# Storing the second sample of the last tile by 16 transfers of falling width

## The chip, the cores and the metric

The kernel runs on one core of one Trainium2 chip. The metric is the device time of one execution in microseconds (us); before the change it is 1864.5 us, the median of two runs (1864.28 and 1864.72). The span in the profile, from the first to the last instruction, is a little shorter: 1862.7 us.

## What is computed

For 1024 samples, `xi` and `xj` each hold 39 fields of 16 numbers. Every one of the 741 pairs (row above column) gets the outer product of two fields, 16 by 16; it is normalised with the mean and variance over all samples and all 256 products of the pair, and multiplied by a 16 by 16 weight.

```python
rows, cols = np.tril_indices(39, k=-1)                       # 741 pairs
cross = xj[:, rows, :, None] * xi[:, cols, None, :]          # 1024 x 741 x 16 x 16
mean = jnp.mean(cross, axis=(0, 2, 3), keepdims=True)
var = jnp.mean(jnp.square(cross - mean), axis=(0, 2, 3), keepdims=True)
normed = (cross - mean) * jax.lax.rsqrt(var + 1e-5)
normed = normed * gamma[None, :, None, None] + beta[None, :, None, None]
out = normed[:, :, None, :, :] * W[None, None, :, :, :]
```

The output is 1024 x 741 x 256 numbers of four bytes, 777 MB; the inputs are 6 MB. So the work is above all the writing of the output.

## The kernel before

Each of the 128 partitions holds eight samples, since 1024 = 128 x 8. A *tile* is `(r, t0, u)`: all `r` pairs of row `r` for two samples `t0` and `t0 + 1` of every partition (`T = 2`), at place `u` of the big buffer `y_sb`. The list `tiles` (lines 68 to 77) starts with row 19, goes on with row 20, and then takes the rows 38 down to 21, each followed by its complement 38 - r, so that a long and a short row together fill one of two slots of `y_sb`. The last tile is row 17 (the complement of row 21), with `t0 = 6`: 17 pairs of 256 numbers, that is 17,408 bytes per sample and partition, two samples, 4352 KB in all.

At the start, moments of the inputs are gathered (lines 351 to 473) and turned into one scale and one shift per pair. Then the loop of line 521 goes over the tiles: `products` (line 178) forms the outer products on ScalarE and GpSimd, line 148 and 150; `finish` (line 271) adds the shift and multiplies with the weight, on VectorE (line 308) and for a share of the pairs on GpSimd (lines 294 and 297); `store` (line 220) sends a tile or a piece of one to memory. All stores are issued by SyncE from one line, 231, so they enter one queue in the order of the program, and each is worked off by the 16 DMA engines, each of which takes its part of every transfer in that order.

What decides how `store` cuts its transfers: rows above 19 (`mid`) have one transfer per sample, in general; rows up to 19 have `step = T`, one transfer for both samples. The last tile is of the second kind, so its 4352 KB leave in one transfer.

SyncE waits before each issue for the engines that wrote the tile. It waits for one thing more: each transfer reports its completion on a semaphore, eight semaphores are handed out in turn, and so the issue of a transfer waits until the transfer eight places before it in the program has landed. At the very end (line 555 in the profile, the end of the program) SyncE waits until all transfers have landed.

Of the kernel before, what the change touches and what calls it, by code (L numbers as in the profile page):

```python
# [41 lines left out]
def tile_pair_outer_batchnorm(  # L42
# [15 lines left out]
    nc = tc.nc  # L58
# [3 lines left out]
    EE = E * E  # L62
# [7 lines left out]
    tiles = [(mid, t0, t0 // T * half // 2) for t0 in range(0, NT, T)]  # L70
# [25 lines left out]
    out_v = out.rearrange("(p t) o n i j -> p t (o n i j)", t=NT)  # L96
# [41 lines left out]
    def view(n):  # L138
        r, _, u = tiles[n]
        return y_sb[:, u : u + T * r, :].rearrange("p (t n) e -> p t n e", t=T)  # L140
# [79 lines left out]
    def store(n, c0, c1, t_from=0, t_to=T):  # L220
        r, t0, _ = tiles[n]
        n0 = first[r]

        whole = n >= len(FIRST_PIECES) and r <= WHOLE
        step = 1 if r > mid and (whole or c1 == r) else t_to - t_from
        for t in range(t_from, t_to, step):
            if whole and step == 1 and t == t_to - 1:
                if c1 < r:
                    continue
                c0 = 0  # L230
            nc.sync.dma_start(  # L231
                out_v[:, t0 + t : t0 + t + step, (n0 + c0) * EE : (n0 + c1) * EE],
                view(n)[:, t : t + step, c0:c1, :].rearrange("p t n e -> p t (n e)"),
            )

    def affine(n, pairs, engines=(nc.scalar, nc.gpsimd)):

# [11 lines left out]
    def weigh(n):  # L249

        y = view(n)
        for c0, c1 in zip(bounds(n), bounds(n)[1:]):
            affine(n, range(c0, min(c1, OWN)), (nc.vector,))
            nc.vector.tensor_tensor(  # L254
                y[:, :, c0:c1, :],
                y[:, :, c0:c1, :],
                w_dve.unsqueeze(1).to_broadcast([P, T, c1 - c0, EE]),
                ALU.mult,
            )
            store(n, c0, c1)  # L260
# [10 lines left out]
    def finish(n):  # L271
# [33 lines left out]
        for t in range(0, T, size):  # L305
            for c0, c1 in zip(bounds(n), bounds(n)[1:]):
                for c in [*range(c0, min(c1, p0)), *range(max(c0, p1), c1)]:
                    stt(  # L308
                        y[:, t : t + size, c, :],
                        y[:, t : t + size, c, :],  # L310
                        t_sb[:, n0 + c : n0 + c + 1],
                        w_dve.to_broadcast([P, size, EE]),
                        ALU.add,
                        ALU.mult,
                    )
                store(n, c0, c1, t, t + size)
# [243 lines left out]
```

## Time and profile before

| what | value |
|---|---|
| time, median of 2 runs | 1864.5 us |
| span in the profile | 1862.7 us |
| written to memory | 776.99 MB |
| busy: VectorE (DVE), ScalarE (ACT), GpSimd (POOL) | 92%, 85%, 83% of the span |
| last store (4352 KB), from issue to landing | 26.0 us |
| end of the last compute instruction | about 1835.4 us |

The page of the profile names work by engine and line. A DMA engine is not an instruction engine: what the 16 DMA engines do is told by the DMA rows (their mean busy share, and GB/s moved). A DMA share of 1.00 means that all 16 were busy; one of them alone gives 0.06. PEclk is of no matter here, since TensorE works in the first slice only.

### The profile page before, as it was taken

What the parts mean: (1) busy time and instruction counts of PE and PEld (TensorE: products, weight loads), DVE (VectorE), ACT (ScalarE), POOL (GpSimd) and SP (SyncE); (2) the same over time, 40 slices, a digit from 0 to 9 for tenths busy, and PEclk for the clock granted to TensorE, in tenths of its full rate; (3) what the DMA queues carried; (4) which work ended last, traced back from release to release, by engine and by line L of the source; (5) the groups of instructions that cost most, each with busy time, mean ns of one, the idle gap of its engine ahead of it and who ended that gap; (6) DMA issues with size and microseconds to landing.
All of it is one profiled execution on the core that took longest, in us unless ns stands there. A gap on an engine that the chain in (4) does not pass through costs nothing.

```text
span 1862.7 us, 9385 instructions
## 1 busy us (share of the span) xinstructions
PE 34.3 (2%) x212; PEld 33.7 (2%) x212; DVE 1714.3 (92%) x2638; ACT 1576.3 (85%) x3130; POOL 1542.9 (83%) x1655
## 2 busy tenths in 40 slices
PE   7000000000000000000000000000000000000000
PEld 7000000000000000000000000000000000000000
DVE  8999889899999999999999999999999999999994
ACT  8999888888888776666898989999999998989891
POOL 9999777787777789999988888888888888888882
PEclk7555555555555555555555555555555555555555
DMA  7999999999999999999999999999999999999998
GB/s 289 396 421 421 430 427 427 429 424 427 424 428 423 424 424 426 427 425 425 420 428 429 428 430 427 426 427 427 427 431 427 426 428 431 428 425 428 428 428 359
DMA packets 55286, 783.60 MB, mean 421 GB/s; under 512 B 4784, under 2 KB 6448, under 8 KB 18096
## 3 DMA queue, kind: packets, MB, share of 16 engines
q1 hardware_dynamic: 54928, 782.53, 99.2%
q14 instruction: 69, 0.57, 0.1%
q10 hardware_dynamic: 288, 0.48, 0.1%
q8 instruction: 1, 0.02, 0.0%
HBM read 6.00 MB, written 776.99 MB: 420 GB/s over the span
## 4 chain that ended last, share of the span: by engine, by line
DMA 53%; ACT 22%; DVE 18%; issue 3%; POOL 1%; PE 0%; SPq 0%; ACTq 0%; DVEq 0%; POOLq 0%
DMA out_dram<-y_sb 53%; ACT y_sb L148 22%; DVE y_sb L308 17%; POOL y_sb L150 1%; DVE y_sb L364 0%; POOL xs L170 0%; POOL y_sb L247 0%; PE ps L401 0%; SPq L231 0%; DVE y_sb L254 0%; ACTq L148 0%; PE ps L379 0%; DVE y_sb L385 0%; DVE y_sb L371 0%; DVE xs L183 0%
## 5 line engine op out<-in xcount | busy, mean ns | idle before, releaser
L308 DVE SCALAR_TENSOR_TENSOR y_sb<-y_sb,st_sb,w_dve 128x512 f32<-128x512 f32 (+1 forms) x2511 | 1653.1, 740 | 113.3 <-issue 95.9
L148 ACT ACTIVATE y_sb<-xs,xj_sb 128x144 f32<-128x144 f32 (+23 forms) x2930 | 1453.0, 586 | 238.2 <-DMA out_dram<-y_sb 181.6
L297 POOL TENSOR_TENSOR y_sb<-y_sb,w_sb 128x2048 f32<-128x2048 f32 (+3 forms) x155 | 517.4, 3343 | 89.1 <-ACT y_sb L292 79.5
L150 POOL TENSOR_SCALAR y_sb<-xs,xj_sb 128x320 f32<-128x320 f32 (+19 forms) x1006 | 557.4, 577 | 9.8 <-DMA out_dram<-y_sb 9.7
L170 POOL TENSOR_TENSOR xs<-xi_sb,st_sb 128x640 f32<-128x640 f32 (+33 forms) x135 | 183.9, 1362 | 178.8 <-ACT y_sb L148 174.5
L294 POOL TENSOR_SCALAR y_sb<-y_sb,st_sb 128x512 f32<-128x512 f32 x291 | 196.8, 692 | 5.1 <-ACT y_sb L148 5.1
L292 ACT ACTIVATE y_sb<-y_sb,st_sb 128x512 f32<-128x512 f32 x160 | 100.2, 708 | 3.8 <-POOL y_sb L150 2.1
L203 POOL TENSOR_TENSOR y_sb<-xs,xj_sb 128x1280 f32<-128x1280 f32 (+2 forms) x24 | 66.7, 2802 | 0.0
L193 DVE TENSOR_TENSOR y_sb<-xs,ps 128x256 f32<-128x256 f32 (+3 forms) x32 | 24.8, 818 | 0.5
L487 PE MATMUL ps<-y_sb 38*128 38x38 f32 (+37 forms) x76 | 16.4, 397 | 2.4 <-DVE y_sb L473 2.4
L487 PEld LDWEIGHTS ps<-y_sb 38*128 38x128 f32 x76 | 16.3, 329 | 2.5 <-POOL y_sb L150 2.5
L150 POOL TENSOR_SCALAR y_sb<-xi_sb,xj_sb 128x304 f32<-128x304 f32 x24 | 11.9, 514 | 0.0
L254 DVE TENSOR_TENSOR y_sb<-y_sb,w_dve 128x2048 f32<-128x2048 f32 (+4 forms) x6 | 10.8, 1840 | 0.5 <-POOL y_sb L247 0.5
L364 DVE TENSOR_REDUCE y_sb<-y_sb 128x38 f32<-128x608 f32 x14 | 10.4, 781 | 0.0
L247 POOL TENSOR_SCALAR y_sb<-y_sb,st_sb 128x512 f32<-128x512 f32 x9 | 7.0, 786 | 2.2 <-ACT y_sb L148 2.2
L245 ACT ACTIVATE y_sb<-y_sb,st_sb 128x512 f32<-128x512 f32 x9 | 6.5, 803 | 0.3 <-ACT y_sb L148 0.3
L361 ACT ACTIVATE y_sb<-xi_sb 128x608 f32<-128x608 f32 x8 | 5.7, 707 | 1.1 <-DMA xi_sb<-in_r_xi_dram 0.7
L361 ACT ACTIVATE y_sb<-xj_sb 128x608 f32<-128x608 f32 x8 | 5.7, 708 | 1.1 <-DMA xj_sb<-in_r_xj_dram 0.6
L379 PE MATMUL ps<-xi_sb,y_sb 128*128 128x152 f32 x40 | 6.1, 302 | 0.0
L379 PEld LDWEIGHTS ps<-xi_sb,y_sb 128*128 128x128 f32 x40 | 5.8, 202 | 0.0
L401 PE MATMUL ps<-y_sb 128*128 128x128 f32 x24 | 5.5, 428 | 1.0 <-POOL y_sb L319 1.0
L401 PEld LDWEIGHTS ps<-y_sb 128*128 128x128 f32 x24 | 5.2, 331 | 1.0 <-POOL y_sb L319 1.0
(43 smaller groups left out, 50.5 us busy)
## 6 DMA issues: line engine op xcount, KB each, us to landing
out_dram<-y_sb SPq DMA_DIRECT2D x16, 3072.0 KB, 21.9
out_dram<-y_sb SPq DMA_DIRECT2D x20, 2432.0 KB, 12.5
out_dram<-y_sb SPq DMA_DIRECT2D x10, 4608.0 KB, 15.2
out_dram<-y_sb SPq DMA_DIRECT2D x12, 3840.0 KB, 20.8
out_dram<-y_sb SPq DMA_DIRECT2D x16, 2816.0 KB, 22.1
out_dram<-y_sb SPq DMA_DIRECT2D x12, 3584.0 KB, 22.9
out_dram<-y_sb SPq DMA_DIRECT2D x12, 3328.0 KB, 24.3
out_dram<-y_sb SPq DMA_DIRECT2D x15, 2560.0 KB, 12.3
```

The lines of the kernel that those rows point to most:

```text
L148: nc.scalar.activation(y, src, AF.Copy, scale=scale)
L150: engine.tensor_scalar(y, src, scale, 1.0, ALU.mult, ALU.mult)
L170: nc.gpsimd.tensor_tensor(xs, xi_sb[:, t0 : t0 + T, 0:r, :], s_sb[:, :, n0 : n0 + r, :].to_broadcast([P, T, r, E]), ALU.mult,)
L193: nc.vector.tensor_tensor(view(n)[:, t].rearrange("p n (i j) -> p n i j", j=E), xs[:, t].unsqueeze(2).to_broadcast([P, r, E, E]), xj_short ...
L203: nc.gpsimd.tensor_tensor(view(n)[:, t].rearrange("p n (i j) -> p n i j", j=E), xs[:, t].unsqueeze(2).to_broadcast([P, r, E, E]), xj_sb[:, ...
L292: nc.scalar.activation(y[:, :, c, :], y[:, :, c, :], AF.Identity, bias=t_c)
L294: nc.gpsimd.tensor_scalar(y[:, :, c, :], y[:, :, c, :], t_c, 1.0, ALU.add, ALU.mult)
L297: nc.gpsimd.tensor_tensor(y[:, :, c0:c1, :], y[:, :, c0:c1, :], w_sb.unsqueeze(1).to_broadcast([P, T, c1 - c0, EE]), ALU.mult,)
L308: stt(y[:, t : t + size, c, :], y[:, t : t + size, c, :], t_sb[:, n0 + c : n0 + c + 1], w_dve.to_broadcast([P, size, EE]), ALU.add, ALU.mult,)
L361: nc.scalar.activation(squares[x][:, t], sources[x][:, t], AF.Square, scale=scales[x])
L379: nc.tensor.matmul(ps, unit, sources[x][:, t0:t1, :, e : e + q], start=e == 0, stop=e + q == E)
L487: nc.tensor.matmul(ps[:, :, first[r] - n0 : first[r] - n0 + r], pick[:, r - 1, :], stq[:, :, 0:r], start=True, stop=True,)
```

## The change

```diff
+            to = out_v[:, t0 + t : t0 + t + step, (n0 + c0) * EE : (n0 + c1) * EE]
+            of = view(n)[:, t : t + step, c0:c1, :].rearrange("p t n e -> p t (n e)")
+            if n < len(tiles) - 1:
+                nc.sync.dma_start(to, of)
+                continue
+            nc.sync.dma_start(to[:, 0], of[:, 0])
+            p0 = 0
+            for p in (8, *range(15, 0, -1)):
+                nc.sync.dma_start(to[p0 : p0 + p, 1], of[p0 : p0 + p, 1])
+                p0 += p
```

For every tile but the last nothing changes. The last tile's one transfer becomes 17: its first sample goes over all 128 partitions at once; its second sample goes in 16 transfers over 8, 15, 14, 13 and so on down to 1 partitions, which together are the 128. The bytes are the same. What it is for: at the end of the kernel the 16 DMA engines do not all finish at the same moment, and transfers that cover fewer partitions than there are engines can give some engines more and some less of the remaining bytes.

More of the change, by code (lines that the diff above doesn't have):

```diff
@@ L230, in store @@
                 c0 = 0
[L231 to L234, printed above, removed]
+            to = out_v[:, t0 + t : t0 + t + step, (n0 + c0) * EE : (n0 + c1) * EE]
[8 more added lines that the diff above has]
+                p0 += p
     def affine(n, pairs, engines=(nc.scalar, nc.gpsimd)):
```

## The prediction

> **What bounds the kernel now.** I began with the page: span, DMA totals, and the chain of work that ended last.
>
> ```profile
> span 1862.7 us, 9385 instructions
> ...
> DMA packets 55286, 783.60 MB, mean 421 GB/s; under 512 B 4784, under 2 KB 6448, under 8 KB 18096
> ...
> q1 hardware_dynamic: 54928, 782.53, 99.2%
> ...
> DMA out_dram<-y_sb 53%; ACT y_sb L148 22%; DVE y_sb L308 17%; POOL y_sb L150 1%; DVE y_sb L364 0%; POOL xs L170 0%; POOL y_sb L247 0%; PE ps L401 0%; SPq L231 0%; DVE y_sb L254 0%; ACTq L148 0%; PE ps L379 0%; DVE y_sb L385 0%; DVE y_sb L371 0%; DVE xs L183 0%
> ```
>
> The queue of stores fills 99.2% of the time of 16 DMA engines: the kernel is bound by them, and compute matters only where it feeds them. The change touches the last tile alone, so I looked at SyncE's waits and its timeline from 1835 us on, and then at a table of the DMA share by stretches of the end.
>
> ```profile
> SPq L555 <- DMA out_dram<-y_sb: 25.6, 1, 25.6
> ```
>
> ```profile
> 1835.56 0.38 SPq L231 DMA_DIRECT2D out_dram<-y_sb  x1
> ```
>
> The last store is issued at 1835.56, and nothing but DMA is left for 25.6 us. Its bytes would need 4352 KB / 428 GB/s = 10.4 us; the rest is backlog in front of it.
>
> ```profile
> 1852.00:1854.20 2.20, 0.00 (x0) 0.00 (x0) 0.00 (x0) 0.00 (x0) 0.00 (x0) 0.50 0.98 419
> 1854.40:1855.40 1.00, 0.00 (x0) 0.00 (x0) 0.00 (x0) 0.00 (x0) 0.00 (x0) 0.50 0.29 122
> 1855.40:1856.80 1.40, 0.00 (x0) 0.00 (x0) 0.00 (x0) 0.00 (x0) 0.00 (x0) 0.50 0.23 99
> 1857.00:1858.30 1.30, 0.00 (x0) 0.00 (x0) 0.00 (x0) 0.00 (x0) 0.00 (x0) 0.50 0.19 80
> 1858.50:1859.10 0.60, 0.00 (x0) 0.00 (x0) 0.00 (x0) 0.00 (x0) 0.00 (x0) 0.50 0.14 58
> 1859.20:1861.10 1.90, 0.00 (x0) 0.00 (x0) 0.00 (x0) 0.00 (x0) 0.00 (x0) 0.50 0.04 18
> 1861.10:1862.70 1.60, 0.00 (x0) 0.00 (x0) 0.00 (x0) 0.00 (x0) 0.00 (x0) 0.50 0.00 0
> ```
>
> The last two numbers of a row are DMA share and GB/s. Up to 1854.2 all 16 engines work; then the share falls to 0.29, 0.19, 0.14 and about one sixteenth, that is to 4, 3, 2 and 1 engines. In the packet records twelve engines finish between 1854.4 and 1854.9, the other four at 1856.8, 1858.4, 1859.2 and 1861.13. A packet of this store is one partition's 17,408 bytes, and takes 0.651 us (428 GB/s / 16 = 26.75 GB/s an engine). The latest engine is thus ten packets behind, and sets the end: it enters the last store at 1861.13 - 16 x 0.651 = 1850.7, the others near 1844.1. If the whole lag were spread over 16 engines, about 5 us could be had; nothing more is at stake on this side. The records do not say which of the 16 the late ones are.
>
> [...]
>
> **The change part by part.** [...]
>
> *Issue.* SyncE issues 16 more transfers. A store issue takes 0.33 to 0.38 us alone and up to 1.2 us straight after another (median 0.382, longest 1.347 in the answer for line 231), so 16 cost 6 to 19 us. SyncE is idle from 1836 on, and the twelve early engines need the second sample only at 1844.1 + 8 x 0.651 = 1849.3. For the first few transfers this is hidden.
>
> *The added waits.* Eight completion semaphores go round; in the built instruction order of the changed kernel every transfer waits for the one eight before it. Numbering the narrow ones 1 to 16: number 7 (10 partitions) waits for the last store of row 21, which the latest engine finishes at 1850.7. Number 8 (9 partitions) waits for the first sample's transfer, and numbers 9 to 16 for numbers 1 to 8. Behind the waiting issue the rest of the narrow transfers are queued on SyncE, 45 of the 128 partitions, and the end of the program waits for them. The first sample is complete when the latest engine has done it: 1850.7 + 8 x 0.651 = 1855.9. From the last packet to SyncE's going on take the end of this run: 1861.13 to 1861.58, 0.45 us. From issue to first packet take a store that found the engines idle:
>
> ```profile
> 66.44 0.37 SPq L231 DMA_DIRECT2D out_dram<-y_sb  x1
> ```
> ```profile
> DMA  9999500099995000000000009999900000999950
> ```
>
> Slices of the second are 0.0375 us from 66.4; work starts in the 25th, 67.3, so 0.86 us. Number 8 therefore moves its first byte at 1855.9 + 0.45 + 0.86 = 1857.2 at the earliest, when twelve engines had long been done in the kernel before.
>
> *What then remains.* [...] Low end, if engines run at full rate: 9 x 0.651 = 5.9, end 1863.1, that is 2.0 us after 1861.13. [...] I take +8: [...]nine issues straight after another, at up to 1.2 us, give nearly the same: 1856.4 + 8 x 1.2 + 0.86 + 0.65 = 1867.5, +6.4. Bytes, compute and the program's last 1.1 us stay: nothing there. Forecast: 1864.5 + 8.0 = 1872.5.
>
> **The rivals.** *No port limit on reads:* only waits and the ramp count. [...] So 1866.5 to 1869.7, say 1868. For it: all rates seen are the engines' own[...]. *The balance works:* the waits are absorbed[...]: -1.4, 1863.1, faster. For it: the lag is real and of this size; against: twelve of 16 engines are early[...], and the wait for the first sample is on the latest engine. *Few engines:* if odd counts fell on the largest power of two that divides them, engine 0 would get 1+15+7+13+3+11+5+9+1+7+3+5+1+3+1+1 = 86 packets, 56 us instead of 5: about 1915. [...]
>
> **How the numbers follow.** Forecast (waits and ports) 0.61; no port limit 0.25; balance 0.10; few engines 0.04. The predicted time is the first case's, 1872.5. The range takes the first two with their bounds, 1865.3 to 1878, and leaves out the last two. Two per cent is 37 us: only few engines reaches it, and a little is kept for the unforeseen: faster 0.01, same 0.94, slower 0.05.
>
> **What would show it.** SyncE should wait before the eighth narrow transfer until about 1856.4, and issue the last one after 1862. Packets of 17,408 bytes should take well over 0.651 us[...], once the second sample starts near 1849; if they stay at 0.65, there is no port limit and the first rival holds. The DMA share should fall below one already before 1854, and the end be one to two engines wide for longer than now. I am wrong if the last packet ends before 1861, or if SyncE issues all 17 without a wait near 1856.

## The result, and the profile after

The changed kernel takes 1874.5 us (1874.25 to 1874.79), 10.0 us more than the 1864.5 us before. The ratio is 1.0055, with a 95% interval from 1.0030 to 1.0079; a second measurement beside the experiments below gives the same ratio, 1.0055 (1.0042 to 1.0067). So the change makes the kernel slower by about half a per cent: little, but well clear of no change.

From the page of the changed kernel: the span, the packets, the store queue, and the chain that ended last.

```profile
span 1873.0 us, 9402 instructions
...
DMA packets 55414, 783.60 MB, mean 418 GB/s; under 512 B 4912, under 2 KB 6576, under 8 KB 18224
...
q1 hardware_dynamic: 55056, 782.53, 98.9%
...
DMA out_dram<-y_sb 52%; ACT y_sb L148 24%; DVE y_sb L314 17%; DVE y_sb L370 1%; POOL y_sb L150 1%; POOL xs L170 0%; POOL y_sb L253 0%; DMA xi_sb<-in_r_xi_dram 0%; DVE y_sb L260 0%; SPq L234 0%; POOL y_sb L300 0%; DVE y_sb L377 0%; ACTq L148 0%; DVE y_sb L391 0%; DVE xs L183 0%
```

The span is 10.3 us longer, the bytes are the same. Packets under 512 bytes went from 4784 to 4912, by 128. These are the 4-byte packets with which each engine reports the end of its share: in the kernel before, the last store has 16 of them, twelve from 1854.42 to 1854.61 and the others at 1856.81, 1858.41, 1859.17 and 1861.12, where its data packets end. One transfer over 16 engines (16 reports) has become the first sample's 16 and one report per partition of the second, 16 + 128: here the transfer over p partitions ran on p engines, with one packet for each. Which of the 16 these are isn't shown.

Where the time went is seen in the DMA rows of the last stretches, first before, then after. The last number is GB/s. A packet counts with all its bytes and its whole duration in the stretch in which it starts, so both the rate and the share (the number before it) are rough where packets are long.

```profile
1849.00:1853.00 4.00, 0.00 (x0) 0.00 (x0) 0.00 (x0) 0.00 (x0) 0.00 (x0) 0.50 0.99 424
1853.00:1857.00 4.00, 0.00 (x0) 0.00 (x0) 0.00 (x0) 0.00 (x0) 0.00 (x0) 0.50 0.48 205
1857.00:1861.00 4.00, 0.00 (x0) 0.00 (x0) 0.00 (x0) 0.00 (x0) 0.00 (x0) 0.50 0.11 48
```

```profile
1849.00:1853.00 4.00, 0.00 (x0) 0.00 (x0) 0.00 (x0) 0.00 (x0) 0.00 (x0) 0.50 0.46 123
1853.00:1857.00 4.00, 0.00 (x0) 0.00 (x0) 0.00 (x0) 0.00 (x0) 0.00 (x0) 0.50 0.60 170
1857.00:1861.00 4.00, 0.00 (x0) 0.00 (x0) 0.00 (x0) 0.00 (x0) 0.00 (x0) 0.50 0.55 122
1861.00:1865.00 4.00, 0.00 (x0) 0.00 (x0) 0.00 (x0) 0.00 (x0) 0.00 (x0) 0.50 0.35 104
1865.00:1869.00 4.00, 0.00 (x0) 0.00 (x0) 0.00 (x0) 0.00 (x0) 0.00 (x0) 0.50 0.25 83
1869.00:1872.00 3.00, 0.00 (x0) 0.00 (x0) 0.00 (x0) 0.00 (x0) 0.00 (x0) 0.50 0.09 23
```

Up to about 1849 the rates agree (447 and 440 GB/s from 1846 to 1849). Then, in the stretch in which twelve engines take up the second sample (they report the first from 1848.73 to 1848.92), 424 GB/s become 123, and the rate never comes back. (With the bytes of each packet spread evenly over its duration, 429 become 151: some of the long packets began just before 1849.) The packet records show it one by one: before, all 256 packets of 17,408 bytes of the last tile take 0.65 to 0.66 us; after, 78 take more than 0.7 us, 21 more than 2 us, and the longest 6.0 us. The 256 together hold an engine for 253.8 us instead of 166.9.

SyncE's timeline and its waits (after 1850 us) show the other half.

```profile
1835.60 15.61 SPq L239 DMA_DIRECT2D out_dram<-y_sb  x7
```
```profile
1859.41 9.26 SPq L239 DMA_DIRECT2D out_dram<-y_sb  x9
```
```profile
SPq L239 <- DMA out_dram<-y_sb: 15.6, 6, 8.2
SPq L561 <- DMA out_dram<-y_sb: 3.2, 1, 3.2
```

Seven narrow transfers are issued by 1851.2; then SyncE waits 8.2 us for the first sample to land, and issues the other nine from 1859.41 on, over 9.3 us, some of them waiting again. Twelve engines had finished everything by 1854.6 in the kernel before.

### The profile page after: what moved, and what is told of

Its sections match the earlier page's. It is cut to its first block, busy times and chain, and to the rows that moved or that the text cites. A ratio compares the mean times of both kernels' runs of the same rounds, so it can differ in the third digit from the quotient of the medians.

```text
span 1873.0 us, 9402 instructions
## 1 busy us (share of the span) xinstructions
PE 33.2 (2%) x212; PEld 32.5 (2%) x212; DVE 1714.3 (92%) x2638; ACT 1576.4 (84%) x3130; POOL 1543.0 (82%) x1655
## 2 busy tenths in 40 slices
DMA packets 55414, 783.60 MB, mean 418 GB/s; under 512 B 4912, under 2 KB 6576, under 8 KB 18224
## 4 chain that ended last, share of the span: by engine, by line
DMA 52%; ACT 24%; DVE 18%; issue 2%; POOL 1%; SPq 0%; ACTq 0%; DVEq 0%; PE 0%; POOLq 0%
DMA out_dram<-y_sb 52%; ACT y_sb L148 24%; DVE y_sb L314 17%; DVE y_sb L370 1%; POOL y_sb L150 1%; POOL xs L170 0%; POOL y_sb L253 0%; DMA xi_sb<-in_r_xi_dram 0%; DVE y_sb L260 0%; SPq L234 0%; POOL y_sb L300 0%; DVE y_sb L377 0%; ACTq L148 0%; DVE y_sb L391 0%; DVE xs L183 0%
```

## The experiments

Every experiment differs from the changed kernel in the transfers of the last tile alone (its compute and all other stores are the same), and every one does the whole computation. Theories: the *waits* (each transfer waits for the one eight before it), the *crowding* (packets of some partitions, neighbouring ones above all, slow each other when they move at the same time; the recorded texts say "ports", which no trace here shows), and the *ramp* (some engines get more packets of the second sample than others; which ones was the author's estimate and isn't shown); the first is a rival to the second as the main cause. Times are medians beside runs of the kernel before on the same chip, which had medians of 1864.08 to 1864.28 us.

| version of the second sample | us | difference | ratio, 95% interval |
|---|---|---|---|
| two: one transfer, 128 partitions | 1864.11 | 0.0 | 1.0000 (0.9991 to 1.0008) |
| slices: waits alone | 1865.65 | +1.6 | 1.0008 (1.0000 to 1.0016) |
| seven: neighbouring partitions alone | 1868.67 | +4.6 | 1.0025 (1.0015 to 1.0034) |
| stride8: every eighth partition | 1872.81 | +8.7 | 1.0048 (1.0034 to 1.0061) |
| again: the changed kernel | 1874.45 | +10.3 | 1.0055 (1.0042 to 1.0067) |
| spread: every fourth partition | 1869.28 | +5.1 | 1.0028 (1.0017 to 1.0039) |
| eleven: ramp, no added wait | 1869.22 | +4.9 | 1.0026 (1.0016 to 1.0036) |
| sixrest: last nine in one | 1871.15 | +6.9 | 1.0037 (1.0023 to 1.0051) |
| relief14, relief15 | 1864.63, 1864.49 | +0.5, +0.3 | 1.0003 (0.9995 to 1.0011), 1.0002 (0.9994 to 1.0010) |
| relieflow: part issued by GpSimd | 1865.30 | +1.0 | 1.0005 (0.9997 to 1.0013) |

**Two transfers instead of one.**

```diff
-            p0 = 0
-            for p in (8, *range(15, 0, -1)):
-                nc.sync.dma_start(to[p0 : p0 + p, 1], of[p0 : p0 + p, 1])
-                p0 += p
+            nc.sync.dma_start(to[:, 1], of[:, 1])
```

> Control: the last tile leaves in two transfers of 128 partitions, one per sample. No narrow transfer, no wait on the first sample's landing[...]. Every theory expects the time of the kernel before, 1864.5 us, within 1 us.

Measured: 0.0. Sending the two samples apart costs nothing; what costs is how the second one is cut.

**The waits without ramp and crowding.**

```diff
-            p0 = 0
-            for p in (8, *range(15, 0, -1)):
-                nc.sync.dma_start(to[p0 : p0 + p, 1], of[p0 : p0 + p, 1])
-                p0 += p
+            w = r * EE // 16
+            for k in range(16):
+                nc.sync.dma_start(to[:, 1, k * w : (k + 1) * w], of[:, 1, k * w : (k + 1) * w])
```

> The second sample goes in 16 transfers again, with the same waits eight back, but each over all 128 partitions and a sixteenth of the row (1088 bytes a partition): the waits without ramp and without crowded ports. Theory of the ports (they cost most of the 10 us): at most +3, since the first sample lands at about 1855.9 and nine quick slices are left: last packet at 1856.4 + 9 x 0.43 + 0.86 + 0.4 = 1861.5, +0.5, and up to 1.2 us per issue would give +7. Theory of the waits alone: most of the +10 stays, +6 to +10.

Measured: +1.6. SyncE's timeline after 1852 us:

```profile
1856.19 4.26 SPq L239 DMA_DIRECT2D out_dram<-y_sb  x9
```

All the waits are there: nine of 16 slices stand behind the landing of the first sample, which releases them at 1856.19 (the prediction had 1856.4 for this), and they are issued in 4.3 us. By themselves the waits cost 1.6 us. The theory that they make most of the 10 us falls.

**The crowding without ramp and added wait.**

```diff
-            for p in (8, *range(15, 0, -1)):
+            for p in (16, 16, 16, 16, 16, 16, 32):
```

> The second sample goes in 7 transfers of 16, 16, 16, 16, 16, 16 and 32 neighbouring partitions: each uses all 16 engines equally (no ramp), and none waits for the first sample[...]. Theory of the ports: packets of 17,408 bytes take well over 0.651 us[...], and the end comes 3 to 9 us after that of the kernel before. Theory of the waits: 0, within 1 us. If only the ramp counts: 0.

Measured: +4.6, within what the crowding was expected to do. The DMA rows of its last stretches, as above:

```profile
1849.00:1853.00 4.00, 0.00 (x0) 0.00 (x0) 0.00 (x0) 0.00 (x0) 0.00 (x0) 0.50 0.34 92
1853.00:1857.00 4.00, 0.00 (x0) 0.00 (x0) 0.00 (x0) 0.00 (x0) 0.00 (x0) 0.50 0.97 222
1857.00:1861.00 4.00, 0.00 (x0) 0.00 (x0) 0.00 (x0) 0.00 (x0) 0.00 (x0) 0.50 0.80 209
1861.00:1865.00 4.00, 0.00 (x0) 0.00 (x0) 0.00 (x0) 0.00 (x0) 0.00 (x0) 0.50 0.24 87
```

The rate falls to 92 GB/s where the kernel before had 424: the hole at 1849 needs neither a ramp nor a wait for the first sample. The seven transfers have 16 reports each (145 small packets from 1843 us on: 16 of an older store, 16 of the first sample, 7 x 16, and one of another queue), so the engines share them evenly; still 61 packets take more than 1 us. How fast 16 neighbouring partitions can be sent isn't told by this: with the bytes spread over each packet's duration the 92 are 140, and late engines still read other partitions in that stretch. Nor does it tell what the neighbours have in common.

**Every eighth partition.**

```diff
-            p0 = 0
+            taken = {}
             for p in (8, *range(15, 0, -1)):
-                nc.sync.dma_start(to[p0 : p0 + p, 1], of[p0 : p0 + p, 1])
-                p0 += p
+                c = 0 if p == 8 else abs(p - 8)
+                i0 = taken.get(c, 0)
+                taken[c] = i0 + p
+                lo, hi = c + 8 * i0, c + 8 * (i0 + p - 1) + 1
+                nc.sync.dma_start(to[lo:hi:8, 1], of[lo:hi:8, 1])
+            assert all(v == 16 for v in taken.values()) and len(taken) == 8
```

> The changed kernel with the same 16 widths in the same order and the same waits[...], but each transfer takes every eighth partition[...]. Theory of the ports:[...] the first sample lands near 1856 to 1857, and the end is +3 to +6 instead of +10. Theory of the waits or of the ramp alone: unchanged, +10.

Measured: +8.7, a miss for both. Packets did get shorter, as the crowding theory had it (none above 2 us, where the changed kernel has 21; 204.4 us in all instead of 253.8), but only 1.6 us of the 10 went. SyncE's timeline after 1856 us:

```profile
1857.68 8.42 SPq L243 DMA_DIRECT2D out_dram<-y_sb  x9
```

The release came 1.7 us earlier than in the changed kernel; the nine last transfers again took more than 8 us to issue. Why so little was won here, and so much more in the next version, isn't shown.

**Every fourth partition.** The place at which each transfer begins was the author's choice, by an estimate of which partitions crowd each other; that isn't shown by any trace.

```diff
-            p0 = 0
-            for p in (8, *range(15, 0, -1)):
-                nc.sync.dma_start(to[p0 : p0 + p, 1], of[p0 : p0 + p, 1])
-                p0 += p
+            for p, lo in (
+                (8, 0), (15, 32), (14, 33), (13, 38), (12, 47), (11, 3), (10, 89), (9, 2),
+                (8, 96), (7, 90), (6, 1), (5, 95), (4, 115), (3, 118), (2, 25), (1, 92),
+            ):
+                hi = lo + 4 * (p - 1) + 1
+                nc.sync.dma_start(to[lo:hi:4, 1], of[lo:hi:4, 1])
```

The changed kernel was run again beside it.

> The changed kernel once more, beside the others of this call: 1874.5 us, +10, as every theory has it.

> Same 16 widths, order and waits as the changed kernel; each transfer takes every fourth partition[...]. Theory that ports, ramp and waits each have a share: below the every-eighth form (1872.8): waits +1.5[...]: so +3 to +6. Theory that neighbouring partitions in a transfer do not matter and the ramp with the waits does it: +8 to +10.

Measured: +5.1, within what was expected, against +10.3 for the changed kernel beside it. Widths, order and waits are the same; only which partitions belong to a transfer differs. So 5.2 us, half of the loss, comes from taking neighbouring partitions together. (Issues that follow a long wait take 0.73 to 0.77 us in this form, against 0.28 to 0.29, which works against it.) SyncE's timeline after 1856 us, and the DMA row of the stretch in which the second sample starts:

```profile
1856.48 7.09 SPq L241 DMA_DIRECT2D out_dram<-y_sb  x9
```
```profile
1849.00:1853.00 4.00, 0.00 (x0) 0.00 (x0) 0.00 (x0) 0.00 (x0) 0.00 (x0) 0.50 0.82 294
```

The rate at 1849 is 294 GB/s, and the release is at 1856.48. The four versions with the same waits form a row: with transfers over all 128 partitions (slices) the release is at 1856.19, over every fourth (spread) at 1856.48, over every eighth (stride8) at 1857.68, over neighbours (the changed kernel) at 1859.41, and at 1858.76 in its second run. The crowding reaches the engine that is late with the *first* sample, and so the wait itself. Distance alone doesn't order the row, since every eighth partition comes out worse than every fourth; what the partitions that slow each other have in common isn't shown.

On which side the crowding lies is open too: partitions that lie together in SBUF also write rows that lie together in memory, and no run changes one without the other. The rates from 1849 to 1853 (123 GB/s over neighbours, 232 in stride8, 294 here) don't tell the two apart.

**The ramp without the added waits.**

```diff
-            p0 = 0
-            for p in (8, *range(15, 0, -1)):
-                nc.sync.dma_start(to[p0 : p0 + p, 1], of[p0 : p0 + p, 1])
-                p0 += p
+            for p0, p1 in ((0, 121), (121, 128)):
+                nc.sync.dma_start(to[p0:p1, 1], of[p0:p1, 1])
```

> The ramp without the added waits: the second sample leaves in two transfers, over 121 partitions[...] and over 7 (7 engines, one each). [...] If the latest engine is a low-numbered one[...]: +2.6[...]. If it is 11 or higher: the end falls to that of a less late engine, -2 to +0.7.

Measured: +4.9. SyncE's waits from 1835 us:

```profile
SPq L559 <- DMA out_dram<-y_sb: 27.7, 3, 20.0
SPq L236 <- DVE y_sb L312: 8.5, 1, 8.5
SPq L559 <- PEq L559: 0.6, 2, 0.4
```

There is no wait before a narrow transfer. In the packet records the engine that ends last works to the end at 0.65 us a packet; it reports the wide transfer at 1865.20, and then does one packet more and reports again at 1865.85. So it is one of those that have a packet of the 7-wide transfer; no trace here shows engine numbers. SyncE's first wait at the end, 20.0 us from 1838.4, puts the landing of the first sample at 1858.4, instead of 1856.2 (slices). How many packets the last engine had is an estimate from these numbers: if the first sample's last packet ended 0.45 us before 1858.4, as in the kernel before, and the same engine then went on to 1865.86, these 7.9 us hold 12 packets at 0.65 us, where an even share of the 128 is 8. The sum is 2.2 us for crowding of the first sample and 2.6 us for four packets more, 4.8, against 4.7 between the last packets of the two traces (1865.86 and 1861.13). By this estimate the engine that ends last here is one of those that this version loads most.

**The last nine transfers in one.**

```diff
-            for p in (8, *range(15, 0, -1)):
+            for p in (8, 15, 14, 13, 12, 11, 55):
```

> The changed kernel's first six narrow transfers (8, 15, 14, 13, 12, 11 partitions, all neighbours), then the remaining 55 partitions in one transfer[...]. No transfer waits for the first sample. [...] If the added waits carry a large share of the 10 us: 3 to 6 us below the changed kernel (+4 to +7). If crowded ports and the ramp do it without them: within 2 us of it (+8 to +10).

Measured: +6.9, at the edge of what a large share of the waits would give. SyncE's waits from 1835 us:

```profile
SPq L561 <- DMA out_dram<-y_sb: 16.3, 2, 9.1
SPq L239 <- DMA out_dram<-y_sb: 8.7, 2, 6.1
```

The 8.2 us wait for the first sample is gone (the two that are left are for older stores), and 3.4 us of the 10.3 with it. That need not be the wait: the packets are shared out otherwise too, one packet is 0.65 us, and how many the last engine had isn't shown for either version. This version doesn't tell the two apart.

**A try at sparing one or two engines.** Both versions send five eighths of each row as ever and cut the rest into 126 and 2 partitions or 120 and 8, which by the author's estimate relieves one or two of the engines; no trace shows which ones.

```diff
-            p0 = 0
-            for p in (8, *range(15, 0, -1)):
-                nc.sync.dma_start(to[p0 : p0 + p, 1], of[p0 : p0 + p, 1])
-                p0 += p
+            w = r * EE * 5 // 8
+            nc.sync.dma_start(to[:, 1, :w], of[:, 1, :w])
+            for p0, p1 in ((0, 126), (126, 128)):        # relief15: (0, 120), (120, 128)
+                nc.sync.dma_start(to[p0:p1, 1, w:], of[p0:p1, 1, w:])
```

> The second sample leaves in three transfers: five eighths of each row over 128 partitions, the last three eighths over the first 126 partitions, and over the last two. [...] No wait on the first sample. [...] If the latest engine is 14: the end comes 1.2 to 1.9 us earlier than in the kernel before (the second latest ended at 1859.2). If it is another: 0 to +0.3.

> [...]the last three eighths go over 120 partitions[...] and over 8 (8 engines, one each)[...]. If the latest engine is 14: the time of the kernel before, 0 to +0.4. If it is 15: 1.2 to 1.9 us faster.

Measured: +0.5 and +0.3, near what was given for "another engine", and not faster. My reading of the changed kernel's trace, that the latest engine has number 14, had no footing: the records carry no engine numbers, and where packets of the same size take from 0.65 to 6.0 us, one can't be matched to the one before it by time alone. So the two runs show only that cutting the rest in these two ways wins nothing.

**A try at a faster version.**

```diff
-            p0 = 0
-            for p in (8, *range(15, 0, -1)):
-                nc.sync.dma_start(to[p0 : p0 + p, 1], of[p0 : p0 + p, 1])
-                p0 += p
+            w = r * EE * 5 // 8
+            nc.sync.dma_start(to[:, 1, :w], of[:, 1, :w])
+            for p0, p1 in ((0, 5), (5, 126), (126, 128)):
+                nc.gpsimd.dma_start(to[p0:p1, 1, w:], of[p0:p1, 1, w:])
```

> A try at a version that beats both: five eighths of the second sample over 128 partitions as ever, the last three eighths issued by GpSimd in three transfers of 5, 121 and 2 partitions. [...] -1 to -1.7 us. If [...]GpSimd's own overhead counts: 0 to several us slower.

Measured: +1.0; it does not beat the kernel before. GpSimd's row of the timeline, and its three transfers in the DMA view (KB each, then us from issue to landing):

```profile
1835.91 1.79 POOL L240 DMA_DIRECT2D out_dram<-y_sb  x3 [6.75 <-DVE y_sb L314]
```
```profile
out_dram<-y_sb POOLq DMA_DIRECT2D x1, 771.4 KB, 17.0
...
out_dram<-y_sb POOLq DMA_DIRECT2D x1, 31.9 KB, 8.2
out_dram<-y_sb POOLq DMA_DIRECT2D x1, 12.8 KB, 17.4
```

The large one has landed by about 1854, while SyncE's stores that were issued before it go on to 1861.9: it did not queue behind them but ran beside them. Which engines it used isn't shown by this trace.

## Why the prediction was right, and where it was off

The forecast was 1872.5, the result 1874.5; direction and case were right, the size was short by 2 of 10 us. Part of this closeness is luck: the +8 was the author's estimate, not worked out from the overlap of the transfers, and a working by issues that came near it (+6.4) was its support; what else it rested on isn't shown by these traces.

*Issue of the first transfers:* right. The first five take about 1.2 us each and are out by 1841.8; number 7 waits for the last store of row 21 and goes at 1850.9 (predicted release 1850.7 + 0.45). A small misreading without effect: twelve engines end from 1854.4 to 1854.6, not to 1854.9.

*The added wait:* right in kind. SyncE does stand before the eighth narrow transfer for the first sample, and the program's end waits for what is queued behind. The rival in which the waits are absorbed and the balance works is out: the time went up.

*"The first sample is complete when the latest engine has done it: 1850.7 + 8 x 0.651 = 1855.9":* this is the term that was mis-sized. I let the second sample's transfers slow each other, and forgot that they can slow the late engine too, which is still on the first sample. The release came at 1859.41 instead of 1856.4, 3.0 us later, and the row of versions above (1856.19, 1856.48, 1857.68, 1859.41) shows that it moves with the partitions that the narrow transfers take together.

*What remains after the release:* right in size. Predicted, with +8, were 12.7 us from 1856.4 to a last packet at 1869.1; measured are 12.2, from 1859.41 to 1871.58. The parts were less right: packets were to take well over 0.651 us, and some took far more than I had thought, up to 6.0 before the release and up to 3.1 after it. The prediction worked this term in two ways, by the packets of an engine and by nine issues one behind the other. The nine issues did take 9.3 of the 12.2 us, and the packet records can be read so that the engine that ends last had a packet at nearly all times from 1864.4 on; no experiment tells which of the two set the end.

*The rival "no port limit on reads"* (+2.0 to +5.2): refuted, as far as narrow transfers read slowly for whatever reason, by the 123 GB/s and by seven and spread. But its upper end is near what the spread form measures, +5.1, where the crowding is less.

*Few engines:* refuted by the 128 added reports. That each engine of a narrow transfer has one packet follows from them; that the same engines have a packet each time, so that some get up to 16 of the second sample, was an estimate that the changed kernel's trace doesn't show.

So the 10.3 us can be laid out in steps between measured versions: waits alone 1.6; from slices to spread 3.5, which I put down to the ramp, with some crowding left and nine issues that take 7.1 us instead of 4.3; crowding 5.2 (again less spread). The steps are not independent: the crowding alone, without ramp and wait on the first sample, cost 4.6, the ramp without added waits 4.9 (2.2 of it crowding), and with crowding the wait for the first sample lasts up to 3.2 us longer (1859.41 against 1856.19). What the change was for was real: the lag of four engines is worth at most some 5 us. It could not be had in this way: the crowding alone costs about as much (4.6 in seven), and the engine that ends last is, by the estimate from eleven, one of those that the narrow transfers load most.

Open: why four engines are late at all, by how much each of the late ones was slowed (the trace has no engine numbers), which engines a narrow transfer takes, which partitions crowd each other, and whether the crowding lies where they are read or at the memory written.

## What to carry to other kernels

Before cutting a transfer into pieces of few partitions, ask three things of it: which engines will run the pieces (the trace shows one report per partition here, so as many engines as partitions), which partitions are then read at once, and which transfer each piece waits for by the reuse of completion semaphores (SyncE stood 8.2 us for the first sample here; in slices, where the waits stand alone, they cost 1.6 us). Pieces that all span 128 partitions and cut the row instead cost 1.6 us where pieces of 1 to 15 neighbouring partitions cost 10. A balance of the tail is only worth trying once it is known which engines are late.

## What was not expected of the hardware

- Crowded packets were not slowed evenly. In the version with seven transfers, twelve packets take 1.27 to 1.29 us, just twice the 0.65, some of them one after another; beside them the ten longest of the first crowd take 4.1 to 5.1 us. Why isn't shown.
- A transfer over every fourth or eighth partition took SyncE longer to issue: the three issues that each follow a long wait (numbers 6 to 8) take 0.73 to 0.77 us in the spread and every-eighth forms, and 0.28 to 0.29 us in the changed kernel, with the same widths.
- GpSimd's transfers went past SyncE's older ones: 17.0 us to landing for a transfer of 771 KB, while the last SyncE store before it, issued at 1835.8, had landed only by 1862.3.
